# A two-layer graph kernel: a chunk order, slot masks on ScalarE, a tenth row buffer, and a last group that reads stored 0/1 rows

## The chip, the cores and the metric

The kernel runs on one NeuronCore of one Trainium2 chip. The metric is the device time of one execution in microseconds (us). The kernel before was run three times for the record: median 2956.14 us, lowest 2926.83, highest 2966.73. One further execution was recorded by the hardware profiler; all durations below are from it.

The engines are called TensorE (PE in the profile; PEld is its weight load), VectorE (DVE), ScalarE (ACT), GpSimd (POOL) and SyncE (SP, which here only issues DMA transfers). Each engine works through its own instructions strictly in order. A wait on one instruction therefore holds all that stands behind it on that engine.

## The reference

There are B = 16 batches with N = 1024 nodes and C = 64 channels. `adj` is a 1024x1024 fp32 matrix per batch. The data set up for it has only 0 and 1 and a diagonal of ones; each node has about 16 neighbours. The computation has two layers.

The first layer thins the lists of neighbours, takes three quantiles per channel over what is left, and puts a small network and a layer norm behind them:

```python
nb = (adj_ > 0) & (~eye)                       # adj_ is adj with ones on the diagonal
m = nb.sum(-1);  rank = cumsum(nb, -1) - 1
skip = where(m > 10, (m + 1) // 2, 1)
removed = nb & (skip > 1) & mask & ((rank + 1) % skip == 0)
adj_ = where(removed | removed.T, 0, adj_)     # dilated graph
agg = sum(w * quantile(x[neighbours in adj_], tau)   # own node included; per channel;
          for tau, w in ((0.25, .25), (0.5, .5), (0.75, .25)))   # linear between order statistics
x1 = layer_norm(x + (relu((x + agg) @ W1 + b1) @ W2 + b2) * mask)
```

The second layer passes messages over `adj` as it was given:

```python
msg = adj @ x1
out = layer_norm(x1 + tanh([x1, msg] @ V1 + c1) @ V2 + c2)
```

## The kernel before, in words

**Groups and stages.** Batches are worked in groups of 2, 4, 4, 4 and 2. Each group passes through three stages. The stages of neighbouring groups are interleaved:

- *Listing* (`list_batch`, L618 to L725; "coming"). For each of the eight 128-row tiles of a batch, SyncE loads the fp32 rows of `adj` (L631), VectorE clears the diagonal block (L632) and writes the 0/1 row tile `nb` in bf16 (L640), and ScalarE counts the neighbours (L643). After four tiles the same four are transposed on TensorE (L666), copied to `nb_t` by ScalarE (L668, a ring of two buffers), and ranked (L673 to L677). `nb` stays until the whole batch has been ranked, sorted by degree and scattered to HBM into `order` by eight GpSimd transfers (L723). Its buffers come from the pool `held`, 9 of them, used round-robin: tile 1 of a batch takes the buffer of tile 0 of the batch before it, and so has to wait for that tile's scatter. (Batch 1 borrows other buffers.)
- *Selecting* (`Chunk`, `ChunkByPE`). The nodes of a group, sorted by degree, are cut into chunks of tiles. A chunk (k, t0, t1, by_pe) holds tiles t0 to t1, whose nodes have at most k neighbours including themselves. Its k slots are filled in one of two ways. With by_pe = 0, VectorE searches the node numbers (`MAX8`/`MATCH_REPLACE8`, L827 and L829), forms `idx`, and GpSimd gathers each slot from HBM (L847). With by_pe = 1, TensorE multiplies one-hot matrices `hot` (built by VectorE, L999) with the nodes' features in three bf16 parts (L1007). Empty slots of such a chunk get a large positive or negative number by a matmul of `pads` with a row `free` of ones and zeros (L1014). `free` says which nodes have no neighbour for slot k: it is built by VectorE (L962) from the nodes' degrees `degs`, which SyncE loads from `order` (L958). Then a sorting network of min/max on VectorE (L883) selects the order statistics. ScalarE and TensorE weight them and apply the first layer's network. VectorE and ScalarE do the layer norm, and x1 goes to HBM in sorted order.
- *Messages* (`messages`, L1046 to L1088; "going"). The second layer of a batch. GpSimd gathers x1 back into the nodes' own order (L1050, tile `x1_n`, two buffers). `adj` is loaded again as fp32 (L1058), transposed on TensorE (L1063) and copied by ScalarE (L1064); L1072 forms the message in fp32, a quarter of the nodes at a time; L1077 to L1085 are the dense layers. `put_out` (L1037) adds the residual, does the layer norm and stores `out`. It is called within the next batch's messages, and once more at the very end for the last batch.

**What sets the order.** The plan goes through all chunks of all groups in the order of the table `CHUNKS`. Beside the selection of one chunk it advances the fill of the next two, the listing of the next group and the messages of the group before, in 24 shares. A scheduler then fixes one order of instructions for each engine. GpSimd's order has all gathers (L847, L1050) and scatters (L723) in one queue. SyncE's has all loads and stores in one.

**The check.** A second code path for inputs that don't fit the tables (for example too many neighbours) stands behind the main one. A tile `amiss` collects signs that the fast result can't be used; it is reduced at the end and decides on the branch. It isn't taken here.

The lines that carry the change:

Of the kernel before, what the change touches and what calls it, by code (L numbers as in the profile page):

```python
# [9 lines left out]
F32 = mybir.dt.float32  # L10
F16 = mybir.dt.float16
BF16 = mybir.dt.bfloat16
I32 = mybir.dt.int32
U8 = mybir.dt.uint8
AF = mybir.ActivationFunctionType
ALU = mybir.AluOpType
# [4 lines left out]
P = 128  # L21
# [320 lines left out]
        low=9,  # L342
# [65 lines left out]


@with_exitstack  # L410
def kernel(
# [37 lines left out]
    upper = const.tile([P, P], F32, name="upper")  # L449
# [3 lines left out]
    off_diag_f = const.tile([P, P], F32, name="off_diag_f")  # L453
    nc.vector.tensor_scalar(off_diag_f, ident, -1.0, 1.0, op0=ALU.mult, op1=ALU.add)
# [13 lines left out]
    nc.gpsimd.iota(bins, pattern=[[-1, BINS]], base=BINS - 1, channel_multiplier=0,  # L468
                   allow_small_or_imprecise_dtypes=True)
# [22 lines left out]
    for n, chunks in CHUNKS.items():  # L492
        most[n] = const.tile([P, n], F32, name=f"most{n}")
        least[n] = const.tile([P, n], F32, name=f"least{n}")
        half[n] = const.tile([P, n], F32, name=f"half{n}")
        place[n] = const.tile([P, n, NP], F32, name=f"place{n}")
        nc.gpsimd.memset(place[n], -100.0)
        for k, t0, t1, by_pe in chunks:
            nc.gpsimd.memset(least[n][:, t0:t1], float(NETS[k]["low"]))
            nc.gpsimd.memset(half[n][:, t0:t1], 0.5 * k - 0.25)  # L500
            if k != KTOP:
                for i, (at, _, _) in enumerate(NETS[k]["places"]):
                    nc.gpsimd.memset(place[n][:, t0:t1, i], float(at))
            if by_pe:
                nc.gpsimd.memset(most[n][:, t0:t1], float(k))
            else:
                for t in range(t0, t1):
                    nc.gpsimd.memset(most[n][:, t:t + 1], float(CAPS[n][t]))
# [34 lines left out]
    def flat(t):  # L543
        return t.rearrange("p a b -> p (a b)")
# [38 lines left out]
    held = sort.enter_context(tc.tile_pool(name="held", bufs=NT + 1))  # L583
# [21 lines left out]
    class Group:  # L605
# [3 lines left out]
        def __init__(self, b0, count):  # L609
# [7 lines left out]
            self.parts = []  # L617

    def list_batch(g, b):

        nbs, gone = [], []

        spare = [nets.tile([P, FMAX], F32, name="slots_a", bufs=3).bitcast(BF16) for _ in range(2)] if b == 1 else []
        for half_b in range(2):
# [3 lines left out]
            for t in range(half_b * HT, (half_b + 1) * HT):  # L628
# [3 lines left out]
                nc.vector.tensor_mul(a[:, blk], a[:, blk], off_diag_f)  # L632
# [28 lines left out]
            for t in range(half_b * HT, (half_b + 1) * HT):  # L661
# [6 lines left out]
                nc.scalar.copy(nb_t, p)  # L668

# [261 lines left out]
    class ChunkByPE(Chunk):  # L931
# [13 lines left out]
        def fill(self):  # L945
# [8 lines left out]
            for q in range(g.count // 2):  # L954

                degs = work.tile([1, 2, P, 1], F32, name="degs", bufs=1)
                for i in range(2):
                    nc.sync.dma_start(degs[:, i], g.order[2 * q + i][at0:at0 + P, N // 2:N // 2 + 1].bitcast(  # L958
                        F32).rearrange("(o p) i -> o p i", o=1))
                free = work.tile([1, 3, 2, P], BF16, name="free", bufs=1)  # L960
                for k in range(low, self.k):
                    nc.vector.tensor_scalar(free[:, k - low], degs[:, :, :, 0], float(k), None, op0=ALU.is_le)  # L962
# [14 lines left out]
                nc.scalar.copy(sums, p[:NT, 0])  # L977

# [110 lines left out]

    def prepare(g):  # L1090
        for b in range(g.b0, g.b0 + g.count):
            yield from list_batch(g, b)

    def finish_group(g):
        for b in range(g.b0, g.b0 + g.count):
            yield from messages(g, b)
# [20 lines left out]
    plan = [(i, c) for i, count in enumerate(GROUPS) for c in CHUNKS[count * NT]]  # L1117
# [59 lines left out]
    for _ in finish_group(groups[len(GROUPS) - 1]):  # L1177
        pass
# [5 lines left out]
    nc.vector.tensor_tensor(amiss, amiss, halves, op=ALU.max)  # L1184
    nc.vector.tensor_reduce(worst, amiss, AX.X, ALU.max)
# [13 lines left out]
    off_diag = work.tile([P, P], BF16, name="off_diag")  # L1199
    nc.vector.tensor_copy(off_diag, off_diag_f)  # L1200
# [190 lines left out]
```

## Time and profile before

| | |
|---|---|
| median of 3 runs | 2956.14 us |
| profiled execution | 2957.26 us |
| its span, first to last instruction | 2955.5 us |
| mean granted TensorE clock | 0.861 |
| VectorE busy | 2350.6 us (80%) |
| TensorE busy | 2251.3 us (76%) |
| GpSimd busy | 1714.8 us (58%) |
| ScalarE busy | 1595.1 us (54%) |
| DMA: bytes moved, mean rate | 263.91 MB, 89 GB/s |
| last selection on VectorE ends | about 2844 us |
| second layer of batch 14 / 15 ends on TensorE | 2908.2 / 2939.6 us |
| last store of `out` issued | 2947.09 us |

How to read it. "Busy" is the time in which an engine executed. The profile's second part cuts the span into 40 slices of 73.9 us and gives the busy tenths of each; PEclk is the clock that was granted to TensorE, in tenths. The view of waits gives, for each engine and line, what ended the idle time before it: microseconds in all, number of times, and the longest. In a timeline a row has its start, its duration, engine, line, operation, output and input with shapes, a count, and in brackets the idle time before it and what ended that. Groups of instructions have busy time and mean nanoseconds behind the first bar, idle time before them behind the second. A busy sum over parallel rows can overlap its neighbours by the length of an instruction's tail.

### The profile page before, as it was taken

To read this page: it belongs to the slowest core of one execution; us is meant where nothing else is said; L and a number is where in the kernel's file an instruction comes from. 1 tells how busy PE (TensorE), PEld (TensorE's weight loads), DVE (VectorE), ACT (ScalarE), POOL (GpSimd) and SP (SyncE) were. 2 spreads that over 40 slices of the span, in tenths; PEclk is the share of its full clock that TensorE was granted. 3 is DMA by queue.
4 is the path that set the end of the run, shared out by engine and by line. 5 is a ranking of instruction groups with operands and counts; after the bars stand their busy time and mean duration, and the time that the engine had idled before them with its cause. 6 is when DMAs were issued, how large, how long until landed. Compare 5 with 4: busy or idle time off the path is not lost. (4 is left out here: it accounts for less than half of the span.)

```text
span 2955.5 us, 62402 instructions
## 1 busy us (share of the span) xinstructions
PE 2251.3 (76%) x23370; PEld 1671.3 (57%) x23480; DVE 2350.6 (80%) x5323; ACT 1595.1 (54%) x4046; POOL 1714.8 (58%) x1486
## 2 busy tenths in 40 slices
PE   4357776678687788878687998885969976789987
PEld 2245554456564666556465776654747654566654
DVE  4368996689899899988698989986989878878741
ACT  8425656655445657754455756641555445334655
POOL 1173673258688475568656576476564776556611
PEclk9778898789888899989788998987969887888969
DMA  4411343333322424242333343223322233122323
GB/s 154 145 38 51 90 120 102 99 107 94 101 72 54 125 71 112 60 126 66 111 94 110 98 124 101 63 62 85 91 78 66 70 97 80 38 71 77 93 72 104
DMA packets 223158, 263.91 MB, mean 89 GB/s; under 512 B 149219, under 2 KB 149890, under 8 KB 222848
## 3 DMA queue, kind: packets, MB, share of 16 engines
q1 hardware_dynamic: 175568, 189.00, 22.4%
q0 software_dynamic: 46080, 70.59, 9.4%
q8 instruction: 186, 3.05, 0.4%
q14 instruction: 124, 1.02, 0.1%
q10 hardware_dynamic: 1200, 0.25, 0.0%
HBM read 217.48 MB, written 46.27 MB: 89 GB/s over the span
## 5 line engine op out<-in xcount | busy, mean ns | idle before, releaser
L847 POOL DMA_INDIRECT slots_a<-in_x_dram,idx x992 | 1399.6, 1411 | 660.5 <-issue 307.2
L1007 PE MATMUL p_slots<-hot,parts 128*64 128x256 bf16 (+1 forms) x12288 | 717.8, 274 | 182.1 <-DVE hot L999 157.3
L1007 PEld LDWEIGHTS <-parts 128*64 128x64 bf16 x12288 | 647.4, 116 | 201.9 <-issue 118.4
L883 DVE TENSOR_TENSOR slots_b<-slots_a 128x256 f32<-128x256 f32 (+13 forms) x552 | 343.9, 638 | 73.7 <-DMA slots_a<-in_x_dram,idx 37.1
L999 DVE TENSOR_SCALAR hot<-val 128x2048 bf16<-128x2048 bf16 x456 | 314.7, 705 | 27.6 <-PE p_slots L1007 21.9
L1050 POOL DMA_INDIRECT x_n<-x,places x128 | 156.3, 1221 | 234.6 <-PE p_z L1077 74.3
L673 PE MATMUL p_rank<-reach,nb_t 128*128 128x128 bf16 (+3 forms) x991 | 186.2, 331 | 138.2 <-ACT nb_t L668 115.2
L723 POOL DMA_INDIRECT order<-nb,places x120 | 138.9, 1157 | 243.1 <-issue 134.0
L1018 ACT COPY slots_a<-p_slots 128x512 f32<-128x512 f32 (+2 forms) x136 | 73.2, 538 | 380.7 <-PE p_slots L1007 304.4
L883 DVE TENSOR_TENSOR slots_a<-slots_b 128x256 f32<-128x256 f32 (+11 forms) x501 | 273.6, 557 | 0.6
L643 ACT ACTIVATE gone<-nb 128x512 bf16<-128x512 bf16 x240 | 149.8, 628 | 175.5 <-DVE nb L640 175.1
L1063 PE MATMUL p_adj<-ident,a 128*128 128x128 f32 x1024 | 199.2, 311 | 53.8 <-DMA a<-in_adj_dram 35.4
L673 PEld LDWEIGHTS <-nb_t 128*128 128x128 bf16 x1024 | 95.4, 106 | 214.8 <-ACT nb_t L668 128.7
L907 PE MATMUL p_g<-ident,terms 128*128 128x128 f32 x904 | 204.6, 332 | 15.9 <-ACT terms L904 15.1
L827 DVE MAX8 key<-code 128x8 f16<-128x1024 f16 x170 | 207.1, 1218 | 2.3 <-issue 0.8
L1072 PE MATMUL p_msg<-adj_t,x_n 128*64 128x128 f32 x2048 | 190.7, 307 | 19.4 <-ACT adj_t L1064 10.6
L883 DVE TENSOR_TENSOR slots_b<-slots_b 128x128 f32<-128x128 f32 (+11 forms) x325 | 196.7, 607 | 0.4
L1064 ACT COPY adj_t<-p_adj 128x512 f32<-128x512 f32 x256 | 149.1, 582 | 71.8 <-PE p_adj L1063 70.3
L907 PEld LDWEIGHTS p_g<-ident,terms 128*128 128x128 f32 x904 | 149.3, 214 | 58.1 <-ACT terms L904 33.0
L675 ACT ACTIVATE gone<-p_rank,s 128x512 bf16<-128x512 f32 x240 | 154.2, 687 | 50.3 <-PE p_rank L673 42.6
L1063 PEld LDWEIGHTS p_adj<-ident,a 128*128 128x128 f32 x1024 | 124.6, 154 | 91.5 <-issue 41.4
L1072 PEld LDWEIGHTS p_msg<-adj_t,x_n 128*64 128x64 f32 x2048 | 128.5, 150 | 83.6 <-issue 37.9
(203 smaller groups left out, 4379.7 us busy)
## 6 DMA issues: line engine op xcount, KB each, us to landing
a<-in_adj_dram SPq DMA_DIRECT2D x256, 512.0 KB
row_p<-order SPq DMA_DIRECT2D x64, 256.0 KB
slots_a<-in_x_dram,idx POOLq DMA_INDIRECT x992
row<-order SPq DMA_DIRECT2D x192, 64.0 KB
row<-order SPq DMA_DIRECT2D x32, 128.0 KB
x_s<-in_x_dram SPq DMA_DIRECT2D x16, 256.0 KB
out_dram<-x_n SPq DMA_DIRECT2D x16, 256.0 KB
nb<-in_x_dram SPq DMA_DIRECT2D x120, 32.0 KB
```

What stands on the lines that cost most here:

```text
L643: nc.scalar.activation(r[:, cols], nb[:, cols], AF.Copy, accum_out=m[:, h, t - half_b * HT:t - half_b * HT + 1])
L673: nc.tensor.matmul(p[:, c * P:], nb_t[:, (h * HT + c) * P:(h * HT + c + 1) * P], reach[:, :HALF - c * P], start=c == 0, stop=c == HT - 1)
L675: nc.scalar.activation(r[:, h * HALF:(h + 1) * HALF], p, AF.Abs, bias=biases[h][:, col], scale=2.0)
L827: nc.vector.max(key[:, t, r:r + 8], code)
L847: nc.gpsimd.indirect_dma_start(out=self.a[:, at[k], t, :], out_offset=None, in_=x_rows, in_offset=bass.IndirectOffsetOnAxis(ap=idx[:, t, k ...
L883: nc.vector.tensor_tensor(view(rb, ra, [(d[0], d[1 + side]) for d in dims]), view(ab, aa, [(d[0], d[1]) for d in dims]), view(bb, ba, [(d[ ...
L907: nc.tensor.matmul(p[:, col], flat(terms[:, i - 1:i + 1]), ident, start=t == h and first + i == 1, stop=t == e - 1 and first + i == places ...
L999: nc.vector.tensor_scalar(hot[:, :, :, e], val, float(inside[at]), None, op0=ALU.is_equal)
L1007: nc.tensor.matmul(p[i * C:(i + 1) * C, o:o + w], g.parts[2 * q + i][:, c, h], hot[:, c, i, :w], start=c == 0 and h == 0, stop=c == NT - 1 ...
L1050: nc.gpsimd.indirect_dma_start(out=x1[:, t], out_offset=None, in_=g.x1[b - g.b0], in_offset=bass.IndirectOffsetOnAxis(ap=places[:, b * NT ...
L1063: nc.tensor.transpose(p[:, j, :], a[:, col:col + P], ident)
L1072: nc.tensor.matmul(p[i * C:(i + 1) * C, 1, :QUART], x1[:, j + i, :], adj_t[:, j + i, :], start=j == 0, stop=j == NT - 2)
```

## The change

Five things are changed.

1. The first group has its own order of chunks, `FIRST`: the 17-slot chunk filled by TensorE comes ahead of the gathered 36-slot chunk, and the others follow in turns.
2. `free` is computed by ScalarE. A matmul with ones adds up the per-block counts `sums` to each node's number of listed neighbours; a Relu of (slot − count) gives a positive number where slot k is empty. The loads `degs` and VectorE's comparisons are gone.
3. `held` has 10 row buffers, not 9.
4. The listing of the last group (batches 14 and 15) stores each transposed tile `nb_t` to HBM (`turned`), and tests with one more VectorE instruction per row tile that `adj` equals its own 0/1 form; two strided loads fetch the diagonal, which has to be 1. Its second layer (`last_messages`) loads the stored bf16 rows in place of `adj`, splits x1 in three bf16 parts, and multiplies with 512 columns at a time; nothing is transposed. The diagonal comes from a matmul of x1 with the identity. The result of the test joins `amiss`.
5. The constants `upper`, `off_diag` and `place` are bf16, not fp32.

```diff
+FIRST = ((17, 4, 6, 1), (36, 0, 1, 0), (16, 6, 8, 1), (23, 1, 2, 0), (15, 8, 10, 1), (19, 2, 4, 0),
+         (12, 12, 15, 0), (13, 10, 12, 1), (10, 15, 16, 0))
...
-    held = sort.enter_context(tc.tile_pool(name="held", bufs=NT + 1))
+    held = sort.enter_context(tc.tile_pool(name="held", bufs=NT + 2))
...
+            if b0 + count == B:
+                self.turned = [hbm.tile([N, N], BF16, name=f"turned{b0 + i}") for i in range(count)]
+                self.plain = const.tile([P, 2, count * NT], F32, name="plain")
     def list_batch(g, b):
+        if g.turned:
+            nc.sync.dma_start(g.plain[:, 1, (b - g.b0) * NT:(b - g.b0 + 1) * NT], bass.AP(
+                tensor=adj.tensor, offset=adj[b].offset, ap=[[N + 1, P], [P * (N + 1), NT], [1, 1]]))
...
-                nc.vector.tensor_mul(a[:, blk], a[:, blk], off_diag_f)
+                if g.turned:
+                    scrap = rows.tile([P, N], BF16, name="nb_t")
+                    col = (b - g.b0) * NT + t
+                    nc.vector.scalar_tensor_tensor(scrap, a, 0.0, a, op0=ALU.is_gt, op1=ALU.is_equal,
+                                                   accum_out=g.plain[:, 0, col:col + 1])
+                nc.vector.tensor_mul(a[:, blk], a[:, blk], off_diag)
...
                 nb_t = rows.tile([P, N], BF16, name="nb_t")
                 nc.scalar.copy(nb_t, p)
+                if g.turned:
+                    nc.sync.dma_start(g.turned[b - g.b0][t * P:(t + 1) * P, :], nb_t)
...
-                degs = work.tile([1, 2, P, 1], F32, name="degs", bufs=1)
-                for i in range(2):
-                    nc.sync.dma_start(degs[:, i], g.order[2 * q + i][at0:at0 + P, N // 2:N // 2 + 1].bitcast(
-                        F32).rearrange("(o p) i -> o p i", o=1))
-                free = work.tile([1, 3, 2, P], BF16, name="free", bufs=1)
-                for k in range(low, self.k):
-                    nc.vector.tensor_scalar(free[:, k - low], degs[:, :, :, 0], float(k), None, op0=ALU.is_le)
...
+                nc.tensor.matmul(p[:1, 1], ones_h[:NT, :1], sums, start=True, stop=True)
+                free = work.tile([1, 3, 2, P], BF16, name="free", bufs=1)
+                for k in range(low, self.k):
+                    nc.scalar.activation(flat(free[:, k - low]), p[:1, 1], AF.Relu, bias=slot[:, k:k + 1],
+                                         scale=-1.0)
...
+    def last_messages(g, b):
+        x1 = work.tile([P, NT, C], F32, name="x1_n")
+        for t in range(NT):
+            nc.gpsimd.indirect_dma_start(
+                out=x1[:, t], out_offset=None, in_=g.x1[b - g.b0],
+                in_offset=bass.IndirectOffsetOnAxis(ap=places[:, b * NT + t:b * NT + t + 1], axis=0))
+        parts = nets.tile([P, NT, 3, C], BF16, name="parts", bufs=4)
+        rest = work.tile([P, NT, C], F32, name="x1_rest", tag="wide", bufs=1)
+        for i in range(3):
+            nc.scalar.copy(parts[:, :, i], x1 if i == 0 else rest)
+            if i < 2:
+                nc.vector.tensor_sub(rest, x1 if i == 0 else rest, parts[:, :, i])
+        p_d = ps_m.tile([P, NT, C], F32, name="p_d", tag="y", bufs=1)
+        for h in range(2):
+            room = nets.tile([P, FMAX], F32, name="slots_a", bufs=3)
...
+            nc.sync.dma_start(nbr_t, g.turned[b - g.b0][h * HALF:(h + 1) * HALF, :].rearrange(
+                "(t p) n -> p t n", p=P))
...
+            for j in range(NT):
+                for i in range(3):
+                    nc.tensor.matmul(p[C:2 * C], parts[:, j, i], nbr_t[:, :, j * P:(j + 1) * P],
+                                     start=j == 0 and i == 0, stop=False)
+            for t in range(HT):
+                nc.tensor.matmul(p[C:2 * C, t * P:(t + 1) * P], x1[:, h * HT + t, :], ident,
+                                 start=False, stop=t == HT - 1)
...
+        nc.vector.tensor_add(x1, x1, b2b_r[:, None, :].to_broadcast([P, NT, C]))
+        nc.vector.tensor_add(x1, x1, p_d)
+        layer_norm(work, x1, x1)
+        nc.sync.dma_start(out[b].rearrange("(t p) c -> p t c", p=P), x1)
...
-    for _ in finish_group(groups[len(GROUPS) - 1]):
-        pass
+    g = groups[len(GROUPS) - 1]
+    for b in range(g.b0, B):
+        last_messages(g, b)
     put_out()
```

## The prediction

> **What bounds the kernel.** The busy line and the slices of the page come first: no engine is full, and VectorE is the fullest over the whole span.
>
> ```profile
> PE 2251.3 (76%) x23370; PEld 1671.3 (57%) x23480; DVE 2350.6 (80%) x5323; ACT 1595.1 (54%) x4046; POOL 1714.8 (58%) x1486
> ...
> DVE  4368996689899899988698989986989878878741
> ...
> PEclk9778898789888899989788998987969887888969
> ```
>
> VectorE idles 2955.5 − 2350.6 = 605 us: about 113 in the first 200 us, 97 behind 2840 us, 395 between, in stages that are 77 to 96% busy. So VectorE paces the middle, broken by waits; what matters is which waits. The waits view names the two that the change aims at (columns: us in all, times, longest).
>
> ```profile
> DVE nb L640 <- DMA order<-nb,places: 105.4, 29, 24.9
> ...
> DVE slots_b L883 <- DMA slots_a<-in_x_dram,idx: 37.1, 5, 22.4
> ```
>
> VectorE's timeline places the second in group 0, between the gathered 36-slot chunk's idx and its data, and the first wherever a 0/1 row tile must wait for a buffer:
>
> ```profile
> 198.20 1.83 DVE L883 TENSOR_TENSOR slots_b<-slots_a 128x768 f32<-128x768 f32 x2 [22.42 <-DMA slots_a<-in_x_dram,idx]
> 203.97 0.42 DVE L883 TENSOR_TENSOR slots_b<-slots_a 128x256 f32<-128x256 f32 x1 [3.95 <-DMA slots_a<-in_x_dram,idx]
> ...
> 1393.95 2.80 DVE L999 TENSOR_SCALAR hot<-val 128x2048 bf16<-128x2048 bf16 x4
> 1420.15 0.93 DVE L640 TENSOR_SCALAR nb<-a 128x1024 bf16<-128x1024 f32 x1 [23.40 <-DMA order<-nb,places]
> ```
>
> GpSimd's timeline of the same moment shows what the 23.40 us are: its queue works through slot gathers at 1.3 us each, then eight gathers of second-layer rows, and only then the scatter that frees the buffer.
>
> ```profile
> 1405.71 0.99 POOL L847 DMA_INDIRECT slots_a<-in_x_dram,idx  x1 [0.31 <-issue]
> 1407.00 0.96 POOL L1050 DMA_INDIRECT x_n<-x,places  x1 [0.30 <-issue]
> ...
> 1417.01 1.01 POOL L723 DMA_INDIRECT order<-nb,places  x1 [0.30 <-DMA x_n<-x,places]
> ```
>
> Behind 2844 us TensorE paces: batch 14's second layer runs 2878 to 2908.2, batch 15's to 2939.6, its layer norm to the last store at 2947.09.
>
> **Order of group 0: −20.** In before, VectorE finishes at 175.8 and stands 22.4 + 4.0 = 26.4 us; only 10 of the 16 one-hot builds stand ahead of it. In the changed order all 16 builds and the whole selection of the 17-slot chunk (some 70 instructions, 25 to 30 us by the shapes' rows) stand between the 36-chunk's idx and its data. The idx comes later, by 6 builds at 0.62 and the key searches displaced, about 5 us, so the 35 gathers end near 209 instead of 203. VectorE reaches that point near 207. Gain 26.4 less 5 = 21, taken as 20; ends 10 and 26.
>
> **ScalarE's `free`: −13.** Eighty VectorE instructions go:
>
> ```profile
> L962 DVE TENSOR_SCALAR free<-degs 1x256 bf16<-1x256 f32 x80 | 20.3, 284 | 1.2 <-PE p_slots L1014 1.2
> ```
>
> They overlap their neighbours by some 0.08, so 80 × 0.2 = 16 to 20 us. Where VectorE paces (85 to 90% busy) some 0.65 of that reaches the end: 11. The 64 `degs` loads leave SyncE's queue, 0.59 us each = 38 us, with 38.4 us of waits for `free` to be read; loads queued behind them come earlier, of which VectorE's 65.1 us of waits for `a` may give back 2. The added 80 ScalarE Relus (1x256; nearest row L977's 8x256 cast, 0.36 us) are 29 us on an engine that is busy 54%; the 32 matmuls at 0.3 are 10 us on TensorE, beside selection work. Ends 0 and −22.
>
> **Tenth row buffer: −10.** It looks like the cure for 105.4 us. But the changed static order says otherwise. Before, tile 1 of each batch stands some 100 rows behind tile 0, waits for the first scatter of the batch before it, and tiles 2 and 3 follow one or two rows later. After, tile 1 stands ahead of the same 100 rows and tile 2 waits for the same scatter at the same place. GpSimd's sequence of gathers and scatters is unchanged in groups 2 to 4 but for a few gathers. So the stall is moved from one tile to the next, and each shrinks only by one tile's VectorE work (0.70 + 0.28 us for L640 and L632): 13 stalls × 1 us = 13, taken as 10. Ends 0 and −50: half of the stalls.
>
> **Last group's check: +15 and +8.** Sixteen 128x1024 scalar_tensor_tensor are new on VectorE; the trace has the shape in selection:
>
> ```profile
> L883 DVE TENSOR_TENSOR slots_b<-slots_a 128x1024 f32<-128x1024 f32 x27 | 32.1, 1216 | 10.6 <-PE p_chosen L1033 4.6 <-ACT terms L904 3.6 <-DMA slots_a<-in_x_dram,idx 2.4
> ```
>
> 16 × 1.2 = 19, at a place (1600 to 2200 us) where VectorE is 68 to 93% busy: 0.8 of it, 15. Their output is a scrap tile in the two-buffer ring of `nb_t`. Five of the sixteen therefore wait until a transposed tile has been stored to HBM, and that store stands in SyncE's one queue. Behind the waiting check on VectorE stand one-hot builds and selections, for which TensorE and the next gathers wait. The queue often stands there (SyncE's waits, 1760 to 2245 us):
>
> ```profile
> SPq L808 <- DVE code L825: 65.6, 5, 32.5
> SPq L966 <- PE p_row L969: 60.1, 6, 21.8
> SPq L631 <- PE p_adj L1063: 32.3, 6, 14.3
> ```
>
> Price of one such wait: nothing, if the store is through, up to 32.5. The nearest VectorE row is the ordinary L640 stall, about 3.5 us, but at some of the five places the store will be long done, so 5 × 1.6 = 8. The two loads of 4-byte diagonal elements issue at about 7 us; the check behind them blocks VectorE by up to 8 us while ScalarE, fully busy from 10 to 80 us, covers it: 0, or 8 uncovered.
>
> **Tail: +7.** Its TensorE work shrinks: no transposes of adj; a half is 24 bf16 matmuls of 512 columns (0.22 us between starts where two of L685 follow each other: 5.2), eight fp32 ones (1.2), copies (1.1), the two dense layers (0.9 + 0.9) and tanh (0.6): 9.9 us, so by TensorE's work alone 61 us become 40. But `x1_n` has two buffers, batch 13's rows keep one until the last `put_out`, and batch 15's rows get batch 14's buffer. Then batch 15's gather waits for batch 14's store, as it did for batch 13's in before, 3.4 us after its issue:
>
> ```profile
> 2886.35 0.39 SPq L1044 DMA_DIRECT2D out_dram<-x_n  x1
> ...
> 2939.61 0.69 DVE L1041 TENSOR_TENSOR x_n<-x_n,b2b_r 128x512 f32<-128x512 f32 x1 [22.00 <-PE p_msg L1072]
> ...
> 2947.09 0.39 SPq L1044 DMA_DIRECT2D out_dram<-x_n  x1
> ```
>
> There the gather hid behind a whole batch of work; now nothing is left to hide it. Batch 14: rows at 2879; three-way split 3.7 (three copies of 0.55, two subtractions of 0.69, hand-overs); two halves of 9.9 → 2902.4; layer norm 7.3 → 2909.7; release 3.4 → 2913; eight gathers at 1.25 and 1.8 to land → 2924.8; split and halves 23.5 → 2948; layer norm 7.5, tangled with batch 13's, +1 → last store near 2956 against 2947.09: +9, and +7 since the halves may overlap. Ends −18 (separate buffers: 61 − 40, less the uneven start) and +12.
>
> A rule and a row on the clock here: after a break of 26.55 us TensorE starts again at 149.69 us; the granted clock is 0.50 to 160, 0.61 to 165, and 1.00 only then, while it is busy 78 to 90%. The Trainium skill ("TensorE: Matmul & The Clock Gate", section "What's actually happening") says that the gate opens after one busy window of about 3.4 us; by the rule a restart costs the batch behind it some 2 us, by the row 5 or more. It speaks against a tail with breaks; the +7 holds without it.
>
> The bf16 constants remove or add nothing that shows: 0, since L632 (0.28) keeps its shape.
>
> **Sum.** −20 − 13 − 10 + 15 + 8 + 7 = −13. Against the profiled execution's 2957.26 that is 2944; the median of the runs shown, 2956.14, lies 1.1 lower. A measurement here tells about 2%, 59 us, from no change.
>
> **Rivals.** *The stalls really go* (0.14, 2880): the tenth buffer takes 50 of the 105 us, group 0 gives 26, and the check hides in the remaining idle time. For it: the two stalls of 23 to 25 us are a single tile's bad luck in GpSimd's queue. Against: the unchanged sequence of scatters. −26 − 13 − 50 + 5 + 7 = −77.
> *No gain* (0.14, 2968): group 0's time is lost again at the first list hand-over, since the scatters there wait for gathers that now start 5 us later; −5 − 5 − 0 + 15 + 0 + 7 = +12.
> *Slower* (0.12, 3040): the checks wait for stores behind SyncE's blocked queue. Five waits of 21 us (mean of 32.5, 21.8, 14.3, 6.7 and 31.2, the longest waits there) = 105, in place of the 8: −21 + 105 = +84. It turns the sign from 21 / 5 = 4.2 us a wait, and passes 2% from 16.
> *The change does not do what it says* is part of the forecast for the tenth buffer and the tail.
>
> The forecast's case has 0.60, with 2905 to 2975 as its own range. The range 2885 to 2992 reaches half-way to the fast case and includes the no-gain case; the slower case is mostly left out. Faster by over 2%: 0.14, slower by over 2%: 0.10 (most of that rival), within: 0.76.
>
> **What the profile after would show.** Right: no wait over 5 us for the 36-chunk's data near 200 us; the wait of 0/1 rows for `order` still 70 to 100 us in all, now on each batch's third tile; TensorE idle for over 15 us between batches 14 and 15, with batch 15's gather a few us behind the store of batch 14; the last store some 110 us behind the last selection instead of 103 (2844 to 2947). Wrong: `order` waits under 50 us; batch 15's gather beside batch 14's work; checks that stand over 10 us for a `turned` store; or stages shifted so that new waits of over 20 us appear which no row here has.

## The result, and the profile after

| | before | after |
|---|---|---|
| median | 2957.72 us (4 runs, 2926.83 to 2966.73) | 2998.75 us (4 runs, 2987.79 to 3003.36) |
| ratio | | 1.014, 95% interval 1.0098 to 1.0182 |
| profiled execution, span | 2957.26, 2955.5 us | 3003.36, 3001.6 us |

In the ratios, here and below, a run more than 1.5% above the fastest run of its kernel is left out. The change costs 41 us. The forecast, 2944 us, was wrong in sign, and the time lies above the range. The page's busy line of after:

```profile
PE 2227.9 (74%) x23097; PEld 1641.6 (55%) x23200; DVE 2351.8 (78%) x5282; ACT 1600.0 (53%) x4062; POOL 1801.1 (60%) x1487
```

VectorE has the same busy time as before (2350.6), so nearly all the loss is idle time on it. GpSimd is 86 us busier (1714.8) with one instruction more: its gathers and scatters have become longer. The view of waits, VectorE's rows (us in all, times, longest):

```profile
DVE nb L658 <- DMA order<-nb,places: 126.7, 28, 35.4
DVE ln_st L559 <- ACT ln_sq L558: 95.1, 27, 31.4
...
DVE slots_b L903 <- DMA slots_a<-in_x_dram,idx: 17.9, 7, 6.1
```

Group 0's wait is mended (37.1 us became 17.9, the longest 22.4 became 6.1). The 0/1 rows wait longer than before (105.4), and the layer norm too (71.8, longest 20.6). VectorE's timeline says where:

```profile
218.59 1.83 DVE L903 TENSOR_TENSOR slots_b<-slots_a 128x768 f32<-128x768 f32 x2 [6.12 <-DMA slots_a<-in_x_dram,idx]
...
788.59 0.69 DVE L658 TENSOR_SCALAR nb<-a 128x1024 bf16<-128x1024 f32 x1 [27.91 <-DMA order<-nb,places]
...
990.57 0.69 DVE L658 TENSOR_SCALAR nb<-a 128x1024 bf16<-128x1024 f32 x1 [35.37 <-DMA order<-nb,places]
...
2041.79 0.22 DVE L559 TENSOR_REDUCE ln_st<-ln_sq 128x1 f32<-128x64 f32 x1 [31.42 <-ACT ln_sq L558]
```

The same rows of before idled 6.91 us (783.75), 8.06 (968.11) and 11.94 (1993.47). The last one has a cause that can be followed upstream: GpSimd, TensorE and ScalarE of after, in order of time (start, duration; in brackets the idle time before it and what ended that), and below them GpSimd, TensorE and VectorE of before at the same place:

```profile
1950.29 32.44 POOL L867 DMA_INDIRECT slots_a<-in_x_dram,idx  x1 [0.30 <-issue]
...
2025.75 0.42 PE L1087 MATMUL p_msg<-ident,x_n 128*64 128x128 f32 x1 [25.27 <-DMA x_n<-x,places]
...
2027.12 1.18 ACT L994 ACTIVATE free<-p_sums,slot 1x256 bf16<-1x256 f32 x3 [26.57 <-PE p_sums L991]
```

```profile
1943.52 5.54 POOL L847 DMA_INDIRECT slots_a<-in_x_dram,idx  x1 [0.30 <-issue]
...
1976.68 0.42 PE L1069 MATMUL p_msg<-ident,x_n 128*64 128x128 f32 x1 [6.05 <-DMA x_n<-x,places]
...
1993.47 0.22 DVE L553 TENSOR_REDUCE ln_st<-ln_sq 128x1 f32<-128x64 f32 x1 [11.94 <-ACT ln_sq L552]
```

One gather takes 32.44 us where the next one takes 1.05; the longest of the same stretch of before takes 5.54. Thirty gathers stand in GpSimd's queue between its last long break and the second layer's rows: from the first of them to the rows it is 47.8 us in before and 78.7 in after. All that stands behind the long gather in GpSimd's queue comes later, so TensorE waits 25.27 us for the second layer's rows (6.05 in before), the ones matmul for `free` stands behind that on TensorE, ScalarE waits for it with the layer norm's squares behind, and VectorE idles 31.42 us. The link through L991 and L994 is new: in before, `free` doesn't pass through TensorE and ScalarE.

### The profile page after: what moved, and what is told of

Same layout as the page of the kernel before. It is cut to its first block, busy times and chain, and to the rows that moved or that the text cites. A ratio compares the mean times of both kernels' runs of the same rounds, so it can differ in the third digit from the quotient of the medians.

```text
span 3001.6 us, 61695 instructions
## 1 busy us (share of the span) xinstructions
PE 2227.9 (74%) x23097; PEld 1641.6 (55%) x23200; DVE 2351.8 (78%) x5282; ACT 1600.0 (53%) x4062; POOL 1801.1 (60%) x1487
## 5 line engine op out<-in xcount | busy, mean ns | idle before, releaser
L867 POOL DMA_INDIRECT slots_a<-in_x_dram,idx x992 | 1453.8, 1465 | 660.3 <-issue 311.7
L903 DVE TENSOR_TENSOR slots_b<-slots_a 128x256 f32<-128x256 f32 (+13 forms) x552 | 343.9, 639 | 57.1 <-ACT terms L924 18.1
L693 PE MATMUL p_rank<-reach,nb_t 128*128 128x256 bf16 (+3 forms) x993 | 196.4, 347 | 143.9 <-ACT nb_t L686 116.5
L903 DVE TENSOR_TENSOR slots_a<-slots_b 128x256 f32<-128x256 f32 (+11 forms) x501 | 273.6, 557 | 0.6
L1068 POOL DMA_INDIRECT x_n<-x,places x112 | 167.9, 1499 | 115.7 <-DMA srt<-order 28.6
L1081 PE MATMUL p_adj<-ident,a 128*128 128x128 f32 x896 | 173.0, 309 | 51.3 <-DMA a<-in_adj_dram 34.8
L927 PE MATMUL p_g<-ident,terms 128*128 128x128 f32 x904 | 195.3, 320 | 10.9 <-ACT terms L924 10.3
L903 DVE TENSOR_TENSOR slots_b<-slots_b 128x128 f32<-128x128 f32 (+10 forms) x325 | 197.1, 608 | 0.5
L1090 PE MATMUL p_msg<-adj_t,x_n 128*64 128x128 f32 x1792 | 170.9, 306 | 30.4 <-DMA x_n<-x,places 20.7
L658 DVE TENSOR_SCALAR nb<-a 128x1024 bf16<-128x1024 f32 x120 | 84.1, 702 | 127.2 <-DMA order<-nb,places 126.7
L1082 ACT COPY adj_t<-p_adj 128x512 f32<-128x512 f32 x224 | 130.8, 584 | 51.5 <-PE p_adj L1081 49.9
L710 ACT ACTIVATE nb<-p_val 128x512 bf16<-128x512 f32 x240 | 143.0, 603 | 25.3 <-PE p_val L708 24.1
```

The lines of the kernel that those rows point to most:

```text
L693: nc.tensor.matmul(p[:, c * P:], nb_t[:, (h * HT + c) * P:(h * HT + c + 1) * P], reach[:, :HALF - c * P], start=c == 0, stop=c == HT - 1)
L867: nc.gpsimd.indirect_dma_start(out=self.a[:, at[k], t, :], out_offset=None, in_=x_rows, in_offset=bass.IndirectOffsetOnAxis(ap=idx[:, t, k ...
L903: nc.vector.tensor_tensor(view(rb, ra, [(d[0], d[1 + side]) for d in dims]), view(ab, aa, [(d[0], d[1]) for d in dims]), view(bb, ba, [(d[ ...
L927: nc.tensor.matmul(p[:, col], flat(terms[:, i - 1:i + 1]), ident, start=t == h and first + i == 1, stop=t == e - 1 and first + i == places ...
L1068: nc.gpsimd.indirect_dma_start(out=x1[:, t], out_offset=None, in_=g.x1[b - g.b0], in_offset=bass.IndirectOffsetOnAxis(ap=places[:, b * NT ...
L1081: nc.tensor.transpose(p[:, j, :], a[:, col:col + P], ident)
```

## The experiments

Unless said otherwise, a run is compared with runs of before on the same chip, and that chip gave before medians of 2954.82 and 2959.69 us. Ratios have their 95% intervals.

**Each part taken out of after.** The old chunk order for group 0:

```diff
-    plan = [(i, c) for i, count in enumerate(GROUPS) for c in (CHUNKS[count * NT] if i else FIRST)]
+    plan = [(i, c) for i, count in enumerate(GROUPS) for c in CHUNKS[count * NT]]
```

> The changed kernel with the old chunk order in group 0 (36-slot chunk first again). Theory 'starved gathers': GpSimd's gathers stretch from 1.0 us to 5 to 32 us where VectorE works without a break on selection and one-hot builds, and the time lost is the VectorE waits that come behind GpSimd's late scatters and second-layer gathers. Then the 26 us hole near 200 us comes back, but the long waits of 27.9, 35.4 and 31.4 us may move, shrink or grow with it: 2970 to 3025 us, and the difference is to be found in the sum of GpSimd's gather durations, not near 200 us alone. Rival 'parts add up': group 0 alone is 20 us worse, everything behind is the same, 3015 to 3020 us.

Measured: 3001.78 us, 1.0126 (1.0065 to 1.0187). The hole is back, 23.8 us at its longest, and the time is that of after. If the new order is worth anything at the end, it is less than these intervals show. Where its gain goes is seen earlier. VectorE and GpSimd of after, then GpSimd of the run with the old order:

```profile
397.73 0.91 DVE L658 TENSOR_SCALAR nb<-a 128x1024 bf16<-128x1024 f32 x1 [18.95 <-DMA order<-nb,places]
```

```profile
393.27 1.00 POOL L867 DMA_INDIRECT slots_a<-in_x_dram,idx  x1 [0.30 <-issue]
394.58 1.03 POOL L743 DMA_INDIRECT order<-nb,places  x1 [0.30 <-issue]
```

```profile
372.45 1.05 POOL L743 DMA_INDIRECT order<-nb,places  x1 [13.99 <-ACT slots_a L1036]
```

With the new order GpSimd goes from gather to gather (about 1.0 us each, 0.30 between) up to 394.58 us, and only then come the scatters that free the buffer for VectorE's next row tile; with the old order GpSimd stands idle before the same scatter, at 372.45. VectorE waits 18.1 to 21.4 us here in all six kernels profiled on this chip with the new order, those with the masks on VectorE and with nine buffers among them, and no more than 3.5 in the three with the old one. So the hole of 22 us near 200 us has become one of 19 us near 400.

Nine row buffers in place of ten:

```diff
-    held = sort.enter_context(tc.tile_pool(name="held", bufs=NT + 2))
+    held = sort.enter_context(tc.tile_pool(name="held", bufs=NT + 1))
```

> The changed kernel with nine row buffers again. Theory 'starved gathers', with the tenth buffer as what lets VectorE run further without a break: the waits of 27.9 and 35.4 us for order fall back towards the 6.9 and 8.1 of before, 2955 to 2975 us. Rival 'parts add up': the tenth buffer saved about 10, so 3005 to 3010 us, with the same long waits one tile earlier.

Measured: 3007.99 us, 1.0154 (1.0108 to 1.02). By the ratios and by the medians the tenth buffer gains 4 and 9 us, less than the intervals can tell from nothing.

The last group as it was (no check, no stored rows, the old second layer):

```diff
-            if b0 + count == B:
+            if False:
...
-    for b in range(g.b0, B):
-        last_messages(g, b)
+    for _ in finish_group(groups[len(GROUPS) - 1]):
+        pass
```

> The changed kernel without the last group's part: no check, no stored rows, second layer of batches 14 and 15 from adj as in before. Theory 'starved gathers': the check's 16 VectorE instructions and the tail go (about -20 and -8), but the waits of 27.9 us near 790 and 35.4 us near 990, which lie ahead of this part's first instruction, stay: 2965 to 2980 us. Rival 'the last group's part is all of the loss': 2945 us or less, below before.

Measured: 2994.04 us (6 runs, 2951.21 to 3006.02), 1.0056 (0.9993 to 1.0119); the ratio takes three of the six. Against after's 1.014 the part costs 0.0084, some 25 us; by the medians of all runs it costs 5. These runs don't settle its price.

**The tail's serial batches.** One call more, which sends batch 13's rows out ahead of batch 14 and so frees its `x1_n` buffer:

```diff
     g = groups[len(GROUPS) - 1]
+    put_out()
     for b in range(g.b0, B):
         last_messages(g, b)
```

> The changed kernel with one more put_out() ahead of the last group's second layer, so that batch 13's rows leave their buffer and batch 15's gather need not wait for batch 14's store. If the shared buffer is what made the tail serial, the gather of batch 15 starts before batch 14's store is issued and the last store comes 18 to 28 us earlier: 2970 to 2980 us. If the tail is bound by something else (TensorE, the loads of the stored rows), less than 8 us change.

Measured: 2975.58 us (10 runs, 2960.67 to 2992.91), 1.007 (1.0038 to 1.0101). In after, GpSimd's timeline has batch 15's gather behind batch 14's store:

```profile
2950.49 0.94 POOL L1113 DMA_INDIRECT x_n<-x,places  x1 [35.77 <-DMA out_dram<-x_n]
```

With the early call that wait is 14.30 us and the gather starts 24.5 us behind batch 14's, not 45.5. From the last x1 store to the last `out` store after takes 8 us longer than before, this kernel 4 us shorter. So 12 of the 23 us between the medians are the tail; the rest lies ahead of it, where the two programs are the same, and shows how far single executions of one program stand apart: 20 us at 1014 us of the span in the two profiles. A difference of up to that size at one place of one profile shows nothing by itself.

**What makes a gather long.** A kernel of its own, run once, on one of the slower chips of below, which computes nothing of the reference but copies x to `out` as a filler: ten gathers of 128 rows, beside a run of one kind of VectorE instruction.

```diff
+    def two(n, i):
+        nc.vector.tensor_tensor(outs[i % 4][:, :n], src[:, :n], other[:, :n], op=ALU.min)
...
+        for k in range(GATHERS):
+            nc.gpsimd.indirect_dma_start(out=got[:, k], out_offset=None, in_=x_rows,
+                                         in_offset=bass.IndirectOffsetOnAxis(ap=idx, axis=0),
+                                         bounds_check=B * N - 1, oob_is_err=False)
+        for i in range(count):
+            op(i)
```

> Not the computation: x is copied to the output, and beside it GpSimd issues ten gathers of 128x64 fp32 in each of eleven stretches, while VectorE repeats one kind of instruction. Theory 'starved gathers': alone 1.0 us each; beside fp32 min of two SBUF tiles (64, 256, 1024 columns) and beside bf16 one-hot builds without a break single gathers take as long as VectorE's unbroken run, tens of us; beside MAX8 and beside a min whose second input is in PSUM about 1.0 to 1.3 us; one short MAX8 behind every seventh min lets each gather through within some 3 us. Rival 'the gathers are long for want of DMA or HBM': 1.0 us in all stretches, as no large transfer runs beside them.

GpSimd's timeline: idle VectorE first, then min of two SBUF inputs of 64, 256 and 1024 columns. The last row is VectorE's run of 64 columns.

```profile
27.68 1.00 POOL L99 DMA_INDIRECT got_idle<-in_x_dram,idx_idle  x1 [0.30 <-issue]
...
44.48 40.18 POOL L99 DMA_INDIRECT got_two<-in_x_dram,idx_two  x1 [0.30 <-issue]
...
99.94 1.04 POOL L99 DMA_INDIRECT got_two<-in_x_dram,idx_two  x1 [0.30 <-issue]
...
142.51 1.96 POOL L99 DMA_INDIRECT got_two<-in_x_dram,idx_two  x1 [0.30 <-issue]
```

```profile
43.02 40.77 DVE L51 TENSOR_TENSOR outs<-src,other 128x64 f32<-128x64 f32 x300
```

Beside 64 columns one of the ten gathers took 40.18 us and ended 0.87 us behind VectorE's run (84.66 and 83.79); the next one took 1.00. Beside 256 columns they took 1.04, beside 1024 columns 1.96. One-hot builds gave 1.05, MAX8 1.00, one input in PSUM 1.00, a reduction 1.00. The stretch nearest to a selection, two minima of 256 columns and a one-hot build in turns, gave 1.00 to 1.31. (Where a short MAX8 was to stand behind every seventh minimum, the ten gathers were through before that pattern began, so the probe says nothing of it.) So the forecast of long gathers held for one of its four kinds of instruction. A gather can be starved by short VectorE instructions with two SBUF inputs; that the mixture of a selection (L903) does it, the probe does not show.

The profiles of the kernels do. In after the long gather ends at 1982.73 us. Beside it each VectorE instruction starts before the one ahead of it has ended, but for one gap of 0.06 us:

```profile
1981.58 0.28 DVE L903 TENSOR_TENSOR slots_a<-slots_b 128x128 f32<-128x128 f32 x1
...
1981.92 1.31 DVE L1017 TENSOR_SCALAR hot<-val 128x2048 bf16<-128x2048 bf16 x2
```

The first of these ends at 1981.86, 0.87 us ahead of the gather's end, as in the probe. Of the 62 gathers over 10 us in the profiles of nine kernels on the chip of before, 61 end 0.85 to 0.91 us behind the end of one VectorE instruction; a time picked at random inside them does so in 16% of the cases. So it is VectorE's stream that holds them and lets them go. Which end of an instruction lets a gather go is not found: most have no gap behind them.

The Trainium skill ("SBUF — State Buffer", section "SBUF: two separate sides") says that VectorE and GpSimd share a pair of SBUF ports under an exclusive lock, and that descriptors which GpSimd writes for its own transfers can be locked out by VectorE; it names fast modes of VectorE as the cause, and for two inputs only an operation of GpSimd that reads SBUF. The 40.18 us look like that lock-out. They came from a condition that it doesn't name for a gather, the one-hot builds didn't bring them (1.05 us), and the dependence on the column count stands in no rule there.

**`free` alone.** The kernel before with the masks on ScalarE and no other edit:

```diff
-                for k in range(low, self.k):
-                    nc.vector.tensor_scalar(free[:, k - low], degs[:, :, :, 0], float(k), None, op0=ALU.is_le)
...
+                nc.tensor.matmul(p[:1, 1], ones_h[:NT, :1], sums, start=True, stop=True)
+                for k in range(low, self.k):
+                    nc.scalar.activation(flat(free[:, k - low]), p[:1, 1], AF.Relu, bias=slot[:, k:k + 1],
+                                         scale=-1.0)
```

> The kernel before with the free-slot masks made on ScalarE from the ones product in PSUM, nothing else, beside a kernel before near 2957 us. If the parts add up as predicted (VectorE loses 160 small instructions), 2940 to 2947 us and GpSimd busy as before (1715 us). If GpSimd's gathers starve where the mask instruction stood on VectorE: 2960 us or more, GpSimd busy over 1740 us, and a gather of 32 us near 1900 to 1960 us of the span that the kernel before has at under 20 us.

Measured: 3022.4 us, 1.0218 (1.02 to 1.0235): 63 us slower, by this edit alone. Its busy line, and the chain from 1950 us on GpSimd, ScalarE and VectorE:

```profile
PE 2305.9 (77%) x23512; PEld 1686.1 (56%) x23512; DVE 2333.3 (77%) x5243; ACT 1632.1 (54%) x4132; POOL 1786.4 (59%) x1487
```

```profile
1953.06 32.52 POOL L850 DMA_INDIRECT slots_a<-in_x_dram,idx  x1 [0.30 <-issue]
...
2030.04 1.18 ACT L978 ACTIVATE free<-p_sums,slot 1x256 bf16<-1x256 f32 x3 [25.70 <-PE p_sums L975]
...
2044.96 0.22 DVE L556 TENSOR_REDUCE ln_st<-ln_sq 128x1 f32<-128x64 f32 x1 [30.25 <-ACT ln_sq L555]
```

VectorE has 80 instructions less (not 160) and works 17.3 us less, as the prediction had it (16 to 20), but from 150 us on it idles 71 us more. The chain is after's, link by link (TensorE's wait for the rows in it is 24.40 us; the thirty gathers take 79.0 us). The edit moves more than the masks, though: the scheduler fixes another order. Of the 5243 instructions that VectorE has in both kernels some 880 stand in another place among the others, of GpSimd's 1486 some 30. No run separates the masks from the order that came with them. A gather of 31.2 to 33.9 us near this place stands in the profiles of all six kernels on this chip that have the masks on ScalarE and no other change to VectorE's selection; before's longest is 19.66, at 2176.86.

The same kernel on three other chips, on which every kernel is slower (before 3846.52, 3811.95 and 3731.79 us):

> The kernel before with only the slot masks moved to ScalarE (no degs loads, no VectorE comparisons). Rival 'parts add up': 10 to 15 us faster, 2940 to 2947 us. Theory 'starved gathers': VectorE loses 80 short instructions that stood between its long runs, GpSimd gets later through, and GpSimd's busy time grows from 1715 to 1740 us or more; with the longest gather from 19.7 to over 30 us the kernel is 5 to 30 us slower.

> The kernel before with only the slot masks on ScalarE, again, on another chip: the first time it ran on a chip where the kernel before itself took 3847 us, with a mean clock of 0.78. If its ratio of 0.985 holds here, 2900 to 2920 us, and 'parts add up' is right for this part. If the mask instructions on VectorE were needed as breaks for GpSimd, 2960 us or more.

> The kernel before with only the slot masks on ScalarE, again. 'Parts add up': 2940 to 2947 us. VectorE's mask instructions were breaks that GpSimd needed: GpSimd busy over 1740 us and 2960 us or more.

Measured: 0.9854 (0.9795 to 0.9914), 0.9938 (0.9894 to 0.9982), 1.0017 (0.9951 to 1.0083). And before with the new chunk order alone, on the same three:

```diff
-    plan = [(i, c) for i, count in enumerate(GROUPS) for c in CHUNKS[count * NT]]
+    plan = [(i, c) for i, count in enumerate(GROUPS) for c in (CHUNKS[count * NT] if i else FIRST)]
```

> The kernel before with only the first group's new chunk order. Rival 'parts add up': the 26 us hole near 200 us is filled and stays so, 2935 to 2940 us. Theory 'starved gathers': VectorE fills the hole, but the gathers that ran through it at 1.0 us each now run beside busy VectorE, so less than 10 us reach the end of group 0 and the rest is lost behind the next late scatter: 2945 to 2965 us.

> The kernel before with only the first group's new order, on the same chip as the others of this call. 'Parts add up': 2930 to 2938 us. 'Starved gathers' (the hole near 200 us was GpSimd's free time, so filling it delays the gathers): 2945 to 2965 us, and the lead that chunks have at 230 to 330 us is gone by the list stage of the next group.

> The kernel before with only the first group's new order, again. 'Parts add up': 2930 to 2938 us. 'Starved gathers': 2945 to 2965 us, with the lead of the first chunks gone by the next group's lists.

Measured: 0.9999 (0.9955 to 1.0043), 1.0012 (0.9956 to 1.0068), 1.0019 (0.9957 to 1.008): nothing, everywhere. GpSimd is 84 to 144 us busier with the masks on ScalarE than with the order alone (1631.8 and 1487.9; 1635.1 and 1507.4; 1641.6 and 1557.4). So the longer gathers come with the masks on every chip (before itself has no profile on these three). Their price doesn't: there VectorE is busy some 62% only, which may leave the same starvation more slack; no run tests that.

**Does the starvation make the whole loss?** If it does, two ways of taking it away should give the time back. First, breaks: the kernel with the early call, and after every sixth short selection step a MAX8 of eight columns whose result isn't used (250 of them).

```diff
+                if i % 6 == 5 and wide <= 384:
+                    nc.vector.max(few, bufs[rb][:, ra, :8])
```

> The changed kernel with the early put_out and, in the selection, a MAX8 of 128x8 behind every sixth min or max of at most 384 columns: 250 more VectorE instructions, some 25 to 35 us of VectorE time. 'Starved gathers': no gather over 10 us is left (before: 19.7, changed: 32.4), GpSimd's busy time falls from 1777 to about 1600 us, and the VectorE waits for order and for the layer norm near 2040 us fall by 40 us or more; net 2940 to 2975 us. Rival 'the long gathers cost nothing, the rest of the queue does': the 25 to 35 us come on top, 2995 to 3010 us.

> The changed kernel with the early put_out and the 250 breaks, again, for a chip on which the kernel before takes its 2955 us (on the chip of the run before, 3812 us, TensorE's instructions issued late and bound the kernel). 'Starved gathers': no gather over 10 us, GpSimd busy about 1600 us, 2940 to 2975 us. Rival 'the long gathers cost nothing': 2995 to 3010 us.

> The changed kernel with the last reply of batch 13 sent out early, and a short MAX8 on VectorE after every sixth selection step of at most 384 columns (250 more VectorE instructions that compute nothing that is used). If short two-input VectorE work starves the gathers and a MAX8 lets them through: no gather over 16 us, GpSimd busy down by 100 us or more from 1777 us, 2940 to 2975 us. If the gathers' length has another cause: the 250 instructions only cost, 2995 to 3010 us.

On two of the slower chips: 0.9708 (0.9612 to 0.9803) and 0.9825 (0.9699 to 0.9952), the fastest kernels measured there; without the breaks this kernel was not run on them. On the chip of the forecast: 2993.7 us, 1.0104 (1.0083 to 1.0125), no faster than without the breaks. No gather over 16 us is left, as forecast, but GpSimd's busy time falls by 77 us and not by 100. The breaks in before:

> The kernel before with the same 250 breaks. 'Starved gathers': GpSimd's busy time falls from 1715 to about 1600 us; before had fewer long gathers on its path, so gain and price about cancel: 2940 to 2970 us. Rival: 2980 to 2990 us.

> The kernel before with the 250 breaks, again. 'Starved gathers': GpSimd busy about 1600 us, 2940 to 2970 us. Rival: 2980 to 2990 us.

Measured on the two slower chips: 1.013 (1.0026 to 1.0235) and 1.0197 (1.0078 to 1.0316), a loss.

Second, the masks back on VectorE, in after with the early call (and with nine row buffers):

```diff
+                for k in range(low, self.k):
+                    nc.vector.tensor_scalar(free[:, k - low], degs[:, :, :, 0], float(k), None, op0=ALU.is_le)
...
-                    nc.scalar.activation(flat(free[:, k - low]), p[:1, 1], AF.Relu, bias=slot[:, k:k + 1],
-                                         scale=-1.0)
```

> The changed kernel with the last reply of batch 13 sent out early, as in the run that had 2975.58 us, and besides with the masks on VectorE from degs again (nine row buffers, for which there is room). If starvation by the moved masks is what lost the time: no gather of 32 us near 1950 us, 2945 to 2962 us. If the masks' move is worth the 13 us gained that were predicted, and the tenth buffer its 4 to 9: 2985 to 2998 us.

Measured: 2989.76 us, 1.0102 (1.0066 to 1.0138). GpSimd's timeline of this kernel at the same place:

```profile
1948.87 17.56 POOL L867 DMA_INDIRECT slots_a<-in_x_dram,idx  x1 [0.30 <-issue]
```

The kernel with breaks has 15.67 us there. Both ways halve the long gather, and GpSimd's busy time falls from 1777.4 us (early call only) to 1720.1 and 1700.1. The time does not follow: both are 9 to 10 us slower by their ratios than the early call only, 14 to 18 by the medians; for the masks on VectorE the missing tenth buffer may be 4 to 9 of it. The 2989.76 us lie in the range that the forecast of this run gave to the −13 of the prediction. So in the changed kernel the place of the masks decides next to nothing, and a theory by which starved gathers are the whole loss falls here. An account of VectorE shows where the sum breaks. Idle is the sum of the brackets in its timeline from 150 us on; busy is from the busy lines.

| kernel | span | VectorE busy | VectorE idle |
|---|---|---|---|
| before | 2955.5 | 2350.6 | 507 |
| after | 3001.6 | 2351.8 | 551 |
| `free` alone | 3013.1 | 2333.3 | 578 |
| after, early call | 2966.3 | 2353.3 | 519 |
| the same, masks on VectorE | 2993.3 | 2369.7 | 525 |
| the same, with breaks | 2992.6 | 2376.4 | 519 |

VectorE's work adds up in every pair: the masks are 16 to 17 us (2350.6 − 2333.3; 2369.7 − 2353.3), the breaks 23, the last group's check 19 to 21 (2369.7 − 2350.6 when `free` is as before; 2331.1 without the last group's part against 2351.8). Idle time does not add up: the masks on ScalarE add 71 us to before's, but take 6 off that of the kernel with the early call. Where the differences to before arise, by the stores of x1 at the same chunk (us; the first column is before's time):

| stretch | after | early call | `free` alone | masks on VectorE | breaks |
|---|---|---|---|---|---|
| to 752.6 | −15 | −28 | +8 | +6 | −15 |
| 752.6 to 827.3 | +16 | +16 | +7 | 0 | +16 |
| 827.3 to 950.1 | −7 | −4 | −2 | −4 | −4 |
| 950.1 to 1014.1 | +30 | +20 | +4 | −3 | +2 |
| 1014.1 to 1929.5 | −2 | +4 | +8 | +5 | +18 |
| 1929.5 to 1997.4 | +27 | +27 | +28 | +14 | +19 |
| 1997.4 to 2864.0 | −10 | −20 | +3 | +24 | +3 |
| to the last store | +8 | −4 | +4 | −4 | −2 |

The three jumps of after, 73 us together, shrink to 11 with the masks back on VectorE: at 750 and 950 us they are gone, and at 1950 us half of one is left, with a gather of 17.56 us. The thirty gathers there take 47.8 us in before and 78.7, 78.8, 79.0, 65.5 and 70.7 in the five kernels of the table, in its order: 31, 31, 31, 18 and 23 us more, beside jumps of 27, 27, 28, 14 and 19. But the lead of group 0 is gone as well, and 24 us are lost behind 1997 us, the larger part of them between 2329 and 2645, where no work is new on VectorE; this loss is not traced, and it is hardly larger than what two profiles of one program differ by. With breaks the jump at 950 us goes, the one at 750 stays, and 18 us go in small pieces between. The jump at 750 is not the new order's: the run with the old order has it too (16 us), and it too leads by 10 us at 752.6.

## Why the prediction was wrong

- **`free`, −13: the step that failed, as an entry of a sum.** The size of the work was right (17 us of VectorE; forecast 16 to 20). That "some 0.65 of that reaches the end" was wrong, and so was its end at 0: alone it is +63 us on this chip. The step priced an instruction of VectorE by its own duration and took idle time for fixed. The edit gave VectorE another stream of instructions, and with it GpSimd other starved gathers, and it put a TensorE product and ScalarE's in-order queue between a late gather and the layer norm. For the 27 us at 1950 us this is shown: by the chain, by the end of the long gather 0.87 us behind a VectorE instruction, and by the thirty gathers, whose length the jump follows in five kernels. The rest of the 63 is not traced to single gathers. A new wait of 19.3 us for `row` at 2446.80 is a part of it, which all kernels of this chip with the masks on ScalarE have and neither of the two with them on VectorE; SyncE's load of `row` stands there 20.8 us for the last batch's scatters. In the changed kernel the step has not been shown to fail: there the masks back on VectorE gain nothing. So the price of this edit depends on the others, a sum of single prices was the wrong form, and how the 41 us divide among the five parts stays open.
- **Order of group 0, −20: wrong in what it brings, the second step that failed.** The hole shrank by 16 us, for 21 forecast (26.4 us to 10.05). At the first list hand-over, near 400 us, it is given back: 18.95 us at 397.73, behind the scatter of 394.58. That is the place and the reason that the rival "no gain" named. The step saw the gathers of group 0 and VectorE's selection, and not that the scatters of the next list stand in the same queue behind those gathers.
- **Tenth row buffer, −10: not refuted** (−4 by the ratios, −9 by the medians, both inside the intervals). The waits for `order` did grow, by 21 us, but not through the buffer: with nine they are 159.2. That a stall moves rather than goes is seen at 2103.16: after waits 24.04 us for the load of `a` where before waits 24.92 and the kernel with nine buffers 23.58 for `order`.
- **Last group, +15 and +8: work right, price open.** The check is 19.5 us of VectorE against 19. The part as a whole, for which 30 were forecast with the tail, costs 25 by the ratios and 5 by the medians. The waits behind stores of `turned`, which carried the +8 and the slower rival, are not there; the check waited for the load of `a` alone, 25.6 us in two pieces, the 24.04 above among them.
- **Tail, +7: right**, in size (+8) and in cause: the gather starts 3.5 us behind the store's issue at 2946.97. The early call undoes it. The last store stands 111 us behind the last selection, for 110 forecast; TensorE's break was 11.5 and then 5.3 us rather than one of 15.
- **Rivals.** "Slower" came true in sign, at half its size and by another mechanism than the one it priced. "No gain" had the loss of group 0's time right, and not the whole. "The stalls really go" is refuted. The sign of wrongness that was named, new waits of over 20 us which no row of before has, is what the profile shows, three times. In the row on the clock, 0.61 is the mean of a stretch in which the clock goes from 0.50 to 1.00; no term rests on it.

What stays open: what the masks cost apart from the new order of instructions; why the idle time that the masks add to before isn't added to the kernel with the early call; where the kernel with the masks back on VectorE loses its 24 us; and which VectorE instruction lets a starved gather go. No kernel was found that beats before on its chip; on the slower chips the early call with breaks does, by 1.8 to 2.9%.

## What to carry to other kernels

When several engines stand in order and one of them paces only 80% of the span, add up busy time and idle time apart. The busy part of an edit can be forecast from a row's duration. The idle part belongs to the whole schedule, and an edit that takes work off the fullest engine can add more idle time than the work was worth (here 71 us against 17). One suspect is another in-order engine between a late transfer and that engine. Look for rows of one instruction whose durations spread (here gathers of 1 to 35 us): they say that something else sets them, and an edit to that something is not priced by its own row. A gain early in the span is kept only if the next hand-over that several engines meet at doesn't wait for something else: here 16 us gained near 200 us became a wait of 19 near 400.

## What was not expected of the hardware

- A gather that GpSimd issues took 1.00 us beside an idle VectorE; beside 64-column two-input minima one of ten took 40.18 us, beside 256 columns all took about 1.04 and beside 1024 about 1.96.
- Nearly every gather over 10 us (61 of 62) ended 0.85 to 0.91 us behind the end of a VectorE instruction.
- Such lengths recur: 32.44, 32.47, 32.51 and 32.52 us in four kernels, on this chip and on a slower one.
- The same edit was worth +2.2% on one chip and between −1.5% and +0.2% on three others, whose before takes 26 to 30% longer.
